# A four-layer graph kernel: the candidate's state product by seven block products, gates blocked by halves of the features, and new figures in its planner

## The chip, the cores and the metric

The kernel runs on one core of one Trainium2 chip, in one launch. The metric is the device time of that launch in microseconds. The core has TensorE (PE; its weight loads are shown apart as PEld), VectorE (DVE), ScalarE (ACT), GpSimd (POOL) and the DMA queues (SP is the queue that issues most loads). TensorE writes to PSUM, which has 8 banks of 128 x 512 fp32 here; the other data lie in SBUF. Everything is fp32.

## The reference

128 graphs of 64 nodes with 256 features pass through four residual layers, each followed by a layer norm. The change is in the first, a gated graph network of five steps with a GRU cell:

```python
for l in range(5):
    m = einsum('bnd,de->bne', h, weight[l])
    agg = einsum('bij,bid->bjd', A, m)          # A = (adj != 0)
    gi = agg @ w_ih.T + b_ih                    # split in i_r, i_z, i_n
    gh = h @ w_hh.T + b_hh                      # split in h_r, h_z, h_n
    r = sigmoid(i_r + h_r); z = sigmoid(i_z + h_z)
    n = tanh(i_n + r * h_n)                     # the candidate
    h = (1 - z) * n + z * h
x = layernorm(x + h * mask)
```

The second layer aggregates, goes from 256 to 1024 features, through an RMS norm and a SiLU, and back to 256; the third aggregates a tangent of the row and projects it onto a ball; the fourth is a small attention over the neighbours. Each is followed by its own layer norm.

## The kernel before

**Tiling.** Two graphs make a block of 128 rows, four blocks a group, and there are 16 groups. A group's state lies with the features on the partitions: `h[:, k, :]` is feature half k (128 features), and the 512 nodes of the group are cut into two halves n = 0, 1 of HR = 256 columns (`half(n)`). `agg` has the same form. The message weight is multiplied into the input weight ahead of time, so aggregation works on h itself.

**The gates** (`gated`, from line 716) are a product of [r; z] weights with [agg; h]. Written as a 2 x 2 block product, the blocks are r and z, agg and h, and the two halves of the nodes. The kernel uses the seven-product scheme (Winograd's form of Strassen's): `a11`, `a12`, `na22` and the weight sums `s1` to `s4` on one side, the sums `t1` to `t4` of values on the other, seven products of 256 x 256 x 256. One such product (`product`, line 656) is four matmuls of 128 x 256. So the gates take 28 matmuls per layer and group instead of 32. The sums t are four VectorE operations of 512 columns (`minus`, line 746), and mix agg with h.

**The candidate** has an input side (`p_in`, weights `w_in`, four matmuls for each half of the nodes) and a state side (`p_hn`, weights `w_hn`, four for each half, eight in all). The state side is computed in `sides(n)` together with the aggregation, and two operations for each half bring it to SBUF as `hnb`, scaled by 0.5 and with half its bias (`scaled`: ScalarE or VectorE). `new_n(n, t)` then makes the candidate of half n from `hnb`, r and `p_in`, and `new_state` the new state.

**The order.** Nothing is issued where it is written. Every operation is recorded in `Flow` with an engine, a booked duration, and what it reads and writes. `Plan.advance` walks a model of the engines, picks at each step the operation that can start first, and `Flow.issue` keeps the best of several plans and emits the instructions in that order; each engine then runs its instructions strictly in order. Operations of several groups stand side by side in it (`WINDOW` = 4 streams; most buffers exist for NF = 3 groups), so one group's matmuls fill another's waiting. The booked figures are:

```python
    HOPS = {"from PE": 0.25, "to PE": 0.3, "else": 0.1}          # L158, a crossing between engines
    def dve(n, run, w, r):
        flow.op("DVE", 0.16 + 0.00105 * n, run, w, r)            # L342
    def act(n, run, w, r):
        flow.op("ACT", 0.27 + 0.00077 * n, run, w, r)            # L345
```

An operation recorded by `either` (`copied`, `scaled`) may go to ScalarE or VectorE; line 99 chooses by start and by how much longer the slower engine takes. Reads and writes are recorded with a part, so `(ps, 0)` and `(ps, 1)` do not wait for each other in the plan. The semaphores themselves are placed by the layer below, from the order in which the instructions are emitted.

**Set-up** (lines 430 to 600) turns the weights, forms the products of the message weights with the input weights (`ps_wmih`), and the weight sums, for layer 0 on VectorE and for layers 1 to 4 on GpSimd.

Of the kernel before, what the change touches and what calls it, by code (L numbers as in the profile page):

```python
# [52 lines left out]
class Plan:  # L53
# [25 lines left out]
    def advance(self, until, rank):  # L79
# [3 lines left out]
        while self.left and clock["PE"] < until:  # L83
            best = None
            for s in range(self.first, min(self.first + flow.WINDOW, len(self.queues))):
                for e, q in self.queues[s].items():
                    opened = False
                    for _, o in zip(range(flow.AHEAD[e]), q):
                        t = max(clock[e], at[o.id])
                        if o.opens is not None:  # L90
                            if opened or not banks or need[o.id]:
                                opened = True
                                continue
                            t = max(t, banks[0])
                        elif need[o.id]:
                            continue
                        elif o.kb and e != "POOL":
                            t = max(t, self.lands[0])
                        key = (t + o.ways[e][0] - min(w[0] for w in o.ways.values()) if len(o.ways) > 1 else t, *rank(s, o))
                        if best is None or key < best[0]:  # L100
                            best = key, o, e, t
# [42 lines left out]
class Flow:  # L144
# [13 lines left out]
    HOPS = {"from PE": 0.25, "to PE": 0.3, "else": 0.1}  # L158
# [55 lines left out]
    def hop(self, e, to):  # L214
        if e == to:
            return 0.0
# [44 lines left out]
def kernel(  # L261
# [79 lines left out]
    def dve(n, run, w, r):  # L341
        flow.op("DVE", 0.16 + 0.00105 * n, run, w, r)  # L342

    def act(n, run, w, r):
        flow.op("ACT", 0.27 + 0.00077 * n, run, w, r)  # L345

    def copied(n, o, i, w, r):

        flow.either([("ACT", 0.27 + 0.00077 * n, lambda: nc.scalar.copy(o(), i())),  # L349
                     ("DVE", 0.16 + 0.00105 * n, lambda: nc.vector.tensor_copy(o(), i()))], w, r)  # L350

    def scaled(n, o, i, scale, bias, w, r):

        flow.either([("ACT", 0.27 + 0.00077 * n, lambda: nc.scalar.activation(o(), i(), AF.Identity, bias=bias(), scale=scale())),  # L354
                     ("DVE", 0.16 + 0.00105 * n, lambda: nc.vector.tensor_scalar(o(), i(), scale(), bias(), OP.mult, OP.add))], w, r)
# [62 lines left out]
    def gate_w(name):  # L418
        return fixed([P, KD, D], name)

    a12, na22, w_hn = gate_w("a12"), gate_w("na22"), gate_w("w_hn")
    a11, s1, s2, s3, s4, w_in = ([gate_w(f"{n}_{l}") for l in range(L)] for n in ("a11", "s1", "s2", "s3", "s4", "w_in"))

# [80 lines left out]
    def hh_out(i, k, ps):  # L504
        if i == 0:
            dve(256, lambda: nc.vector.tensor_copy(a12[:, k, :], ps[:, :D]), [(a12, k)], [ps])
            dve(256, lambda: nc.vector.tensor_scalar(na22[:, k, :], ps[:, D:], -1.0, None, OP.mult), [(na22, k)], [ps])
        else:
            dve(256, lambda: nc.vector.tensor_copy(w_hn[:, k, :], ps[:, :D]), [(w_hn, k)], [ps])
# [10 lines left out]
    for l in range(L):  # L520
# [9 lines left out]
        a21 = unit("AB"[l % 2], S, f"a21_{l}", (P, KD, D))  # L530
        for k in range(KD):
            for i, n in ((0, 2 * D), (1, D)):
# [5 lines left out]
                for dst, at in (((a11[l], 0), (a21, D)) if i == 0 else ((w_in[l], 0),)):  # L538
                    act(256, lambda ps=ps, k=k, dst=dst, at=at: nc.scalar.copy(dst[:, k, :], ps[:, at:at + D]),
                        [(dst, k)], [ps])  # L540

        def sums(e, us, l=l, a21=a21):
            v = nc.vector if e == "DVE" else nc.gpsimd
            for o, x0, x1 in ((s1[l], a21, na22), (s2[l], s1[l], a11[l]), (s3[l], a11[l], a21), (s4[l], a12, s2[l])):
                flow.op(e, us, lambda o=o, x0=x0, x1=x1: v.tensor_sub(o.tile(), x0.tile(), x1.tile()), [o], [x0, x1])
        sums("DVE", 0.7) if l == 0 else sums("POOL", 1.32)
# [5 lines left out]
    m11, m12, mn22, ms1, ms2, ms3, ms4 = range(7)  # L552
# [59 lines left out]
    def group(g):  # L612
# [104 lines left out]
        def gated(l, h):  # L717
# [5 lines left out]
            def sides(n):  # L723
# [5 lines left out]
                p_agg = aggregate(agg, hr, 2 * n, n)  # L729
                p_hn = bank("p_hn")  # L730
                product(p_hn, w_hn, lambda k: h[:, k, half(n)], True, True, (h, n))
                for c in range(KD):
                    scaled(300, lambda c=c: hnb[:, c, half(n)], lambda c=c: p_hn[:, c * HR:(c + 1) * HR], lambda: 0.5,
                           lambda c=c: half_b[:, 2 * KD + c:2 * KD + c + 1], [(hnb, (n, c))], [p_hn, half_b])
                return p_agg
# [3 lines left out]
            t1, t2, t3, t4 = (tA, 0), (tA, 1), (tB, 0), (tB, 1)  # L739
            a = agg  # L740

            def view(t):
                return t[0][:, t[1] * KD:(t[1] + 1) * KD, :]

            def minus(o, x0, x1, r):
                dve(512, lambda: nc.vector.tensor_sub(view(o), x0(), x1()), [o], r)  # L746

            def of(t, n):
                return lambda: t[:, :, half(n)]

            def k_of(t, n):
                return lambda k: t[:, k, half(n)]

            def k_view(t):
                return lambda k: t[0][:, t[1] * KD + k, :]
# [35 lines left out]
            sides(0)  # L791
            product(p1, a11[l], k_of(a, 0), True, False, (a, 0))
            copied(420, lambda: uu.tile(), lambda: blocks_of(p1.tile()), [uu], [p1])
            product(p_in[0], w_in[l], k_of(a, 0), True, True, (a, 0))
            product(p1, a12, k_of(h, 0), False, True, (h, 0))
            tanh_half(ur, lambda c: p1[:, c * HR:(c + 1) * HR], 0, p1)
            new_n(0, ur)
            p_a2 = sides(1)

            a2 = lambda: blocks_of(p_a2.tile())
            minus(t1, a2, of(a, 0), [p_a2, (a, 0)])
            minus(t2, of(h, 1), lambda: view(t1), [(h, 1), t1])
            minus(t3, of(h, 1), a2, [(h, 1), p_a2])
            minus(t4, lambda: view(t2), of(h, 0), [t2, (h, 0)])
            product(pu, s2[l], k_view(t2), True, True, t2)
            plus(uu, pu, uu)
            product(pv, s3[l], k_view(t3), True, False, t3)
            plus(uv, pv, uu)  # L810
            product(pw, s1[l], k_view(t1), True, False, t1)
            product(pv, na22, k_view(t4), False, True, t4)
            plus(uv, pw, uv)
            plus(uz, pv, uu)
            product(pw, s4[l], k_of(h, 1), False, True, (h, 1))
# [4 lines left out]
            product(p_in[1], w_in[l], k_of(a, 1), True, True, (a, 1))  # L820
# [166 lines left out]
        dve(1250, series, [n2, ser, near], [xn])  # L987
# [4 lines left out]
        for b in range(NB):  # L992
            flow.either([
                ("DVE", 0.37, lambda b=b: nc.vector.tensor_scalar(tan[:, b, :], x2[:, b, :], fac[:, b:b + 1], None, OP.mult)),
                ("ACT", 0.47, lambda b=b: nc.scalar.activation(tan[:, b, :], x2[:, b, :], AF.Identity, scale=fac[:, b:b + 1]))],
# [29 lines left out]
        dve(800, onto_ball, [th, un], [th, un, urn])  # L1025
# [14 lines left out]
        for b in range(NB):  # L1040
            ps = bank("ps_a")
            for k in range(KD):
# [5 lines left out]
                ("ACT", 0.47, lambda ps=ps, b=b: nc.scalar.activation(  # L1048
                    hw[:, b, :D], ps[:, :D], AF.Identity, scale=hw[:, b, D:D + 1])),
                ("DVE", 0.43, lambda ps=ps, b=b: nc.vector.tensor_scalar(  # L1050
# [52 lines left out]
```

## Time and profile before

| | |
|---|---|
| time, median of 3 | 2431.84 us (2430.58 to 2432.48) |
| span of the profiled run | 2430.5 us, granted TensorE clock 0.994 |
| TensorE busy | 2394.7 us, 12,258 matmul records |
| VectorE busy | 1893.4 us, 4,097 instructions |
| ScalarE busy | 1147.1 us, 2,408 instructions |
| GpSimd busy | 188.2 us |
| `p_hn` matmuls (state side) | 1,280 records |
| `hnb` from PSUM, on ScalarE / VectorE | 232 x 472 ns / 88 x 480 ns |
| HBM traffic | 25.74 MB read, 8.39 MB written |

An fp32 matmul of 128 x 256 stands as two records in the trace, so records are twice the program's matmuls for that shape. A row of the page names the output and inputs by the program's names without their numbers (`p_w<-tA,s` is a product of a t sum with an s sum). The page's "idle before" is the time an engine stood ahead of the instructions of a row, with what released it.

### The profile page before, as it was taken

The page shows a single profiled execution, that of the slowest core. Times are in us where ns is not written, and L with a number is a line of the kernel's source. Part 1 is how long each engine was busy: PE and PEld are TensorE (multiplying, and loading weights), DVE is VectorE, ACT ScalarE, POOL GpSimd, SP SyncE. Part 2 cuts the span into 40 slices and gives each one's busy share as a digit, 9 for nine tenths or more (in the row PEclk, how much of TensorE's full clock was granted, in tenths as well). Part 3 has the DMA queues.
Part 4 walks back from the last instruction along what each step waited for, and adds up shares of the span by engine and source line. Part 5 has one row for each costly group of instructions (what it writes and reads, how often), then busy time and mean ns, then how long its engine had stood idle before and what let it go on. Part 6 is the DMA issues. An engine that isn't in the chain of part 4 may idle for free.

```text
span 2430.5 us, 32703 instructions
## 1 busy us (share of the span) xinstructions
PE 2394.7 (99%) x12258; PEld 2102.9 (87%) x12258; DVE 1893.4 (78%) x4097; ACT 1147.1 (47%) x2408; POOL 188.2 (8%) x144
## 2 busy tenths in 40 slices
PE   9999999999999999999999999999999999999995
PEld 7888888888888888888888888888888888888864
DVE  3668787887888877778777887888787787878777
ACT  4434544444444444454444545455444544445453
POOL 4000000000100000000000100000000000000011
PEclk9999999999999999999999999999999999999997
DMA  4000000000000000000000000000000000000000
GB/s 127 3 1 12 1 29 1 18 12 1 29 1 27 3 18 11 1 27 3 16 14 1 29 1 27 3 19 11 1 29 1 18 12 1 27 9 18 9 9 18
DMA packets 39725, 36.21 MB, mean 15 GB/s; under 512 B 9956, under 2 KB 38656, under 8 KB 39568
## 3 DMA queue, kind: packets, MB, share of 16 engines
q1 hardware_dynamic: 37840, 32.25, 4.2%
q8 instruction: 97, 1.59, 0.3%
q10 hardware_dynamic: 1328, 1.31, 0.2%
q0 software_dynamic: 400, 0.57, 0.1%
q14 instruction: 60, 0.49, 0.1%
HBM read 25.74 MB, written 8.39 MB: 14 GB/s over the span
## 4 chain that ended last, share of the span: by engine, by line
PE 94%; DVE 4%; ACT 1%; DMA 1%; issue 0%; POOL 0%; SPq 0%; POOLq 0%; ACTq 0%; DVEq 0%
PE p_v L663 11%; PE p_w L663 11%; PE p_in L663 11%; PE p_r L663 11%; PE p_hn L663 11%; PE ps_o L333 9%; PE ps_agg L333 6%; PE p_u L663 6%; PE ps_hr L643 3%; PE ps_a L333 2%; PE p_wh L882 2%; PE p_vh L882 2%; PE p_1h L882 2%; PE ps_T L633 1%; PE ps_att L333 1%; PE p_uh L882 1%
## 5 line engine op out<-in xcount | busy, mean ns | idle before, releaser
L663 PE MATMUL p_hn<-hT,w_hn 128*128 128x256 f32 x1280 | 322.8, 380 | 0.0
L663 PE MATMUL p_in<-agg,w_in 128*128 128x256 f32 x1280 | 315.4, 379 | 0.0
L663 PEld LDWEIGHTS p_in<-agg,w_in 128*128 128x128 f32 x1280 | 240.2, 190 | 31.1
L663 PEld LDWEIGHTS p_hn<-hT,w_hn 128*128 128x128 f32 x1280 | 227.9, 191 | 22.7
L333 PE MATMUL ps_o<-w2s,hid 128*128 128x256 f32 x1024 | 231.2, 379 | 0.0
L333 PEld LDWEIGHTS ps_o<-w2s,hid 128*128 128x128 f32 x1024 | 193.9, 190 | 27.3 <-issue 1.2
L678 POOL TENSOR_TENSOR rstd<-ve,pow 128x4 f32<-128x4 f32 (+1 forms) x64 | 82.5, 1289 | 1491.6 <-DVE ve L676 1484.0
L767 ACT ACTIVATE V<-V,half_b 128x256 f32<-128x256 f32 x160 | 72.7, 500 | 199.2 <-DVE V L763 199.0
L663 PE MATMUL p_u<-tA,s 128*128 128x256 f32 x640 | 158.1, 381 | 1.4 <-DVE tA L746 0.6
L663 PE MATMUL p_w<-tA,s 128*128 128x256 f32 x640 | 158.1, 379 | 0.0
L663 PE MATMUL p_r<-hT,a 128*128 128x256 f32 x640 | 156.9, 379 | 0.0
L663 PE MATMUL p_r<-agg,a 128*128 128x256 f32 x640 | 156.7, 379 | 0.0
L663 PE MATMUL p_v<-tB,s 128*128 128x256 f32 x640 | 155.4, 379 | 0.0
L663 PE MATMUL p_v<-tB,na 128*128 128x256 f32 x640 | 154.5, 379 | 0.0
L663 PE MATMUL p_w<-hT,s 128*128 128x256 f32 x640 | 154.3, 379 | 0.0
L349 ACT COPY agg<-ps_agg 128x512 f32<-128x512 f32 x154 | 89.9, 584 | 114.2 <-PE ps_agg L333 98.8
L333 PEld LDWEIGHTS ps_agg<-edge,hr 128*128 128x128 f32 x1024 | 136.1, 191 | 6.6
L354 ACT ACTIVATE hnb<-p_hn,half_b 128x256 f32<-128x256 f32 x232 | 101.6, 472 | 81.4 <-PE p_hn L663 67.4
L333 PE MATMUL ps_agg<-edge,hr 128*128 128x128 f32 x1024 | 138.8, 275 | 0.0
L663 PEld LDWEIGHTS p_u<-tA,s 128*128 128x128 f32 x640 | 119.3, 190 | 21.0 <-DVE tA L746 2.3
L663 PEld LDWEIGHTS p_v<-tB,s 128*128 128x128 f32 x640 | 120.9, 190 | 16.3 <-PE ps_att L333 0.2
L663 PEld LDWEIGHTS p_w<-hT,s 128*128 128x128 f32 x640 | 120.7, 190 | 16.0
(233 smaller groups left out, 4686.5 us busy)
## 6 DMA issues: line engine op xcount, KB each, us to landing
x<-in_x_dram SPq DMA_DIRECT2D x16, 512.0 KB, 3.6
xr<-in_x_dram SPq DMA_DIRECT2D x16, 512.0 KB, 3.6
out_dram<-x_n SPq DMA_DIRECT2D x16, 512.0 KB, 2.9
edge<-in_adj_dram SPq DMA_DIRECT2D x32, 64.0 KB, 2.3
wm<-in_L_gnn_weight_dram SPq DMA_DIRECT2D x5, 256.0 KB, 5.3
w2s<-in_L_gnn_W_dram SPq DMA_DIRECT2D x1, 1024.0 KB, 10.0
w<-in_L_gnn_W_dram SPq DMA_DIRECT2D x2, 512.0 KB, 3.5
w_in_L_gnn_w_hh_dram<-in_L_gnn_w_hh_dram ACTq DMA_DIRECT2D x1, 512.0 KB, 5.2
```

The source lines that it names most:

```text
L333: return nc.tensor.matmul(o, lhsT, rhs, start=(k == 0), stop=(k == nk - 1))
L349: flow.either([("ACT", 0.27 + 0.00077 * n, lambda: nc.scalar.copy(o(), i())), ("DVE", 0.16 + 0.00105 * n, lambda: nc.vector.tensor_copy(o( ...
L354: flow.either([("ACT", 0.27 + 0.00077 * n, lambda: nc.scalar.activation(o(), i(), AF.Identity, bias=bias(), scale=scale())), ("DVE", 0.16 ...
L633: turn(lambda j=j, c=c: nc.tensor.transpose(ps[:, c * HR + j * P:c * HR + (j + 1) * P], src[:, 2 * n + j, c * P:(c + 1) * P], ident.tile() ...
L643: turn(lambda j=j, c=c: nc.tensor.transpose(ps[:, j * D + c * P:j * D + (c + 1) * P], src[:, c, (2 * n + j) * P:(2 * n + j + 1) * P], iden ...
L663: pe(256, lambda c=c, k=k: nc.tensor.matmul(ps[:, c * HR:(c + 1) * HR], w[:, k, c * P:(c + 1) * P], v(k), start=first and c == k == 0, sto ...
L678: pool(1.1, lambda: nc.gpsimd.tensor_tensor(rstd[:, :m, :], ve[:, :m, :], pow2[:, :m, :], OP.pow), [rstd], [ve])
L767: act(256, lambda c=c: nc.scalar.activation(o[:, c, :], src(c), AF.Tanh, bias=half_b[:, i * KD + c:i * KD + c + 1], scale=0.5), [(o, c)], ...
L882: pe(256, lambda c=c: nc.tensor.matmul(ps[:, c * HR:(c + 1) * HR], w1f[:, w, (2 * q + c) * P:(2 * q + c + 1) * P], v[0](), start=first and ...
```

## The change

There are three parts.

1. **The state side by seven block products.** The weights `w_hn` (256 x 256) are kept as seven 128 x 128 blocks: four blocks (`m11`, `m12`, `mn22` with its sign turned, and one that is overwritten by the fourth sum) and the sums `ms1` to `ms4`, all scaled by 0.5 already. The values are cut by feature half and node half, and the sums `t1` to `t4` of h alone. Seven matmuls take the place of eight. They share two banks, `p_hx` and `p_hy`, in two halves each, and are joined in SBUF by VectorE: two sums with what is in `hs`, and three outputs with sum and bias in one operation.
2. **The gates are blocked by halves of the features.** In the 2 x 2 form the inner blocks are now the feature halves k, each with both agg and h, in place of agg and h. A product is still four matmuls, two from h (`w_h`) and two from agg (`w_a`). For that the sums are formed on h and agg apart: eight of 256 columns in place of four of 512. The sums of h are the ones that the state side needs. Because the sums of h need both halves of the state, and the outputs for node half 0 come partly at the end of the seven, `new_n(0)` now follows the whole of `state_side`.
3. **The planner's figures.** Booked durations of VectorE and ScalarE come down, crossings go up, an operation that follows another on its own engine is booked with a crossing too, and an operation that may go to either engine is booked on VectorE only with 0.4 us added to its start in the comparison.

```diff
-                        key = (t + o.ways[e][0] - min(w[0] for w in o.ways.values()) if len(o.ways) > 1 else t, *rank(s, o))
+                        key = (t + flow.SOONER if len(o.ways) > 1 and e == "DVE" else t, *rank(s, o))
...
-    HOPS = {"from PE": 0.25, "to PE": 0.3, "else": 0.1}
+    HOPS = {"from PE": 0.3, "to PE": 0.3, "else": 0.2, "own": 0.12}
+    SOONER = 0.4
...
-            return 0.0
+            return 0.0 if e == "PE" else self.HOPS["own"]
...
-        flow.op("DVE", 0.16 + 0.00105 * n, run, w, r)
+        flow.op("DVE", 0.105 + 0.00105 * n, run, w, r)
...
-        flow.op("ACT", 0.27 + 0.00077 * n, run, w, r)
+        flow.op("ACT", 0.15 + 0.00077 * n, run, w, r)
...
-    a12, na22, w_hn = gate_w("a12"), gate_w("na22"), gate_w("w_hn")
-    a11, s1, s2, s3, s4, w_in = ([gate_w(f"{n}_{l}") for l in range(L)] for n in ("a11", "s1", "s2", "s3", "s4", "w_in"))
+    m11, m12, mn22, ms1, ms2, ms3, ms4 = range(7)
+    w_h, w_hn = fixed([P, 7, D], "w_h"), fixed([P, 7, P], "w_hn")
+    w_a, w_in = [fixed([P, 7, D], f"w_a_{l}") for l in range(L)], [fixed([P, KD, D], f"w_in_{l}") for l in range(L)]
+    def sums_of(w, eng, us):
+        for o, x0, x1 in ((ms1, ms4, mn22), (ms3, m11, ms4), (ms2, ms1, m11), (ms4, m12, ms2)):
+            flow.op(eng, us, lambda o=o, x0=x0, x1=x1: v.tensor_sub(w[:, o, :], w[:, x0, :], w[:, x1, :]),
...
-                p_hn = bank("p_hn")
-                product(p_hn, w_hn, lambda k: h[:, k, half(n)], True, True, (h, n))
-                for c in range(KD):
-                    scaled(300, lambda c=c: hnb[:, c, half(n)], lambda c=c: p_hn[:, c * HR:(c + 1) * HR], lambda: 0.5, ...
+            def sums(x, i):
+                for o, x0, x1 in ((of(t1), at(0, 1), at(0, 0)), (of(t2), at(1, 1), of(t1)),
+                                  (of(t3), at(1, 1), at(0, 1)), (of(t4), of(t2), at(1, 0))):
+                    dve(256, lambda o=o, x0=x0, x1=x1: nc.vector.tensor_sub(o[0](), x0[0](), x1[0]()), ...
+            def gate(ps, m, v, first, last):
+                for i, w in ((1, w_h), (0, w_a[l])):
+                    for c in range(KD):
+                        pe(256, lambda i=i, w=w, c=c: nc.tensor.matmul(
+                            ps[:, c * HR:(c + 1) * HR], w[:, m, c * P:(c + 1) * P], v[i][0](), ...
+            def state_side():
+                px, py = bank("p_hx"), bank("p_hy")
+                prod(px, 0, m11, block(0, 0), True)
+                copied(256, su[0], lambda: px[:, :HR], [su[1]], [(px, 0)])
+                prod(px, 0, m12, block(1, 0))
+                scaled(256, out(0, 0)[0], lambda: px[:, :HR], lambda: 1.0, lambda: b(0), [out(0, 0)[1]], [(px, 0), half_b])
+                prod(px, 1, ms2, sum_of(t2))
+                plus(su, px, 1, su)
+                prod(py, 0, ms3, sum_of(t3), True)
+                plus(sv, py, 0, su)
+                prod(py, 1, ms1, sum_of(t1))
+                prod(py, 0, mn22, sum_of(t4))
+                plus(out(0, 1), py, 0, su, 1)
+                plus(out(1, 1), py, 1, sv, 1)
+                prod(py, 1, ms4, block(1, 1))
+                plus(out(1, 0), py, 1, su, 0)
...
-            sides(0)
-            product(p1, a11[l], k_of(a, 0), True, False, (a, 0))
+            agg_of(0)
+            gate(p1, m11, block(0, 0), True, False)
             copied(420, lambda: uu.tile(), lambda: blocks_of(p1.tile()), [uu], [p1])
-            product(p1, a12, k_of(h, 0), False, True, (h, 0))
+            gate(p1, m12, block(1, 0), False, True)
             tanh_half(ur, lambda c: p1[:, c * HR:(c + 1) * HR], 0, p1)
+            sums(h, 1)
+            state_side()
+            product(p_in[0], w_in[l], lambda k: agg[:, k, half(0)], True, True, (agg, 0))
             new_n(0, ur)
-            p_a2 = sides(1)
-            minus(t1, a2, of(a, 0), [p_a2, (a, 0)])
+            agg_of(1)
+            sums(agg, 0)
...
-        dve(1250, series, [n2, ser, near], [xn])
+        dve(1150, series, [n2, ser, near], [xn])
```

Some fixed bookings of single operations (`series`, `onto_ball`, `tan`, `hw`) change in the same way; what they compute does not.

## The prediction

> **What bounds the kernel now.** I read the page's busy shares first, then the chain of waits that ended last, then a table of stretches, and last a few microseconds of the timeline.
>
> ```profile
> PE 2394.7 (99%) x12258; PEld 2102.9 (87%) x12258; DVE 1893.4 (78%) x4097; ACT 1147.1 (47%) x2408; POOL 188.2 (8%) x144
> ...
> PE 94%; DVE 4%; ACT 1%; DMA 1%; issue 0%; POOL 0%; SPq 0%; POOLq 0%; ACTq 0%; DVEq 0%
> ...
> L663 PE MATMUL p_hn<-hT,w_hn 128*128 128x256 f32 x1280 | 322.8, 380 | 0.0
> ```
>
> TensorE is busy for 99% of the span and 94% of the closing chain runs over it. The state's product for the candidate (p_hn) never waits: its last column, idle before, is 0.0. The other products of line 663 show 0.0 too, or 1.4.
>
> ```profile
> core 0: us, PE busy (x) PEld busy (x) DVE busy (x) ACT busy (x) POOL busy (x), PEclk, DMA share, GB/s
> ...
> 400.00:1000.00 600.00, 599.29 (x3111) 532.62 (x3110) 484.35 (x1045) 283.67 (x596) 42.74 (x29) 1.00 0.04 12
> ...
> 2300.00:2430.50 130.50, 101.00 (x414) 73.84 (x413) 99.45 (x277) 62.63 (x125) 18.58 (x13) 0.88 0.04 13
> ```
>
> In the body TensorE stands 0.7 us of 600 at full clock; nearly all its idle time is in the last 130 us (29.5) and the first 61 (3.4). Busy time can hide gaps, since records overlap, so I read the pitch:
>
> ```profile
> 2311.04 1.89 PE L663 MATMUL p_u<-tA,s 128*128 128x256 f32 x8
> ...
> 2312.77 1.89 PE L663 MATMUL p_v<-tB,s 128*128 128x256 f32 x8
> 2312.97 0.69 DVE L763 TENSOR_TENSOR U<-p_u,U 128x512 f32<-128x512 f32 x1 [1.07 <-PE p_u L663]
> ...
> 2314.50 1.89 PE L663 MATMUL p_w<-tA,s 128*128 128x256 f32 x8
> ```
>
> Eight records are four matmuls of the program (two records each: p_hn has 1280 records for 16 groups x 5 layers x 8 matmuls). They start 1.73 us apart, so one 128x256 matmul takes 1.73 / 4 = 0.432 us of TensorE, not the 0.380 of one record. I went through all start-to-start steps and took off the shortest of each shape: 38.7 us are left over, 4.2 in the first 61 us, 22.2 in the last 122 and 12.3 in the 2,250 between. The kernel is bound by TensorE's issue, and a matmul removed from the body is worth its pitch.
>
> **What the Trainium skill says.** "Perfetto Trace Analysis", section Identifying the Most-Contended Engine, says that matmul busy time is no good measure of headroom and to use the weight loads' busy share. Here that is 87%, not 99%; the pitch explains it, since a load takes 0.190 us in a step of 0.216. The same page, Engine Utilization, halves TensorE's rate for fp32 done as low and high parts; the two records per matmul agree. The page "PSUM — Partial Sum Buffer", section PSUM bank collisions, says that two engines must not touch the same bank in the same partitions at once, whichever columns they use, so that their accesses have to be ordered by bank. The trace shows such ordering: two evictions of different halves of one p_hn bank wait for each other,
>
> ```profile
> ACT hnb L354 <- DVE hnb L355: 13.0, 16, 2.7
> ...
> DVE hnb L355 <- ACT hnb L354: 8.5, 20, 1.3
> ```
>
> 36 times and 21.5 us in all. This matters below: the new code keeps two products in the two halves of one bank, and the planner books those halves apart.
>
> **The change, part by part.** Counts come from the two built programs, engine by engine.
>
> *TensorE.* The state side goes from 8 matmuls of 128x256 per layer and group to 7: 80 layers (16 x 5) lose one each, 6,676 to 6,596 in all. 80 x 0.432 = **34.6 us**. The gates stay at 28 matmuls a layer; they are only cut another way, and each still loads its own weights, 0.190 hidden under a step of 0.216. Rows of equal instructions rise from 2,538 to 3,394 because gate products now alternate between w_h and w_a; nothing in the timeline charges for a change of weights, so I take 0.
>
> *VectorE.* Removed: 320 sums of 512 (the four tA/tB groups of line 746: 59.4 + 57.9 + 54.9 + 54.5 = 226.7 us) and 88 evictions of hnb (88 x 0.480 = 42.2). Added: 640 sums of 256, nearest the page's line 878 at 0.42 us (268.8); 160 sums of 256 out of PSUM, not seen before: below them 0.42 (line 959's eviction), above 0.48 (line 1028), I take 0.42 (67.2); 240 sums with a bias column, 0.42 to 0.48, I take the upper, as hnb took it (115.2). Net +182. The planner now starts an either-engine operation on VectorE only if that is 0.4 us sooner, and the program shows what moves to ScalarE: 120 x_n (x 0.409), 28 hr (x 0.69), 40 tan (x 0.29), 27 hw (x 0.484), some 9 copies of 512 (x 0.69): −99. VectorE goes to about 1,976 us, 82% of the new span.
>
> *ScalarE.* Loses 232 hnb (101.6), gains 80 at 0.47, 79 copies of 256 at 0.375, the 120 x_n at 0.55, 40 tan at 0.47, 27 hw at 0.47 and 36 copies at 0.58: about +84, to 1,231 us or 51%. Neither engine is full; beside TensorE this costs nothing unless it comes late.
>
> *New waits on TensorE.* The seven products come back three times to a bank that has just been read: m12 after the copy, mn22 after su becomes sv, ms4 after the output of line b(1). Such a return takes from TensorE's last step to VectorE's start 0.20 us (2312.77 to 2312.97 above), 0.42 to 0.48 for the operation, and about 0.06 back (a tA sum that ended at 1655.79 let p_u start at 1655.85): 0.70 us. What stands behind a waiting matmul is all of TensorE's queue, so a late one costs its lateness in full. What hides it is other groups' work placed between by the planner, which books 0.6 us for the two crossings and is aware of these three. It is not aware of the bank: its parts (px, 0) and (px, 1) are free of each other, yet the program's semaphores order them. Counting in the program's order, 297 matmuls into p_hx or p_hy follow a read of the other half; 52 have about 1 us of matmuls or less between, where a return takes 0.70 or more when VectorE is not free at once. At 0.1 us each I take **5 us**; bounds 0 and 30 (all 297 at 0.1). Some 370 VectorE reads also wait for a matmul into the other half, up to 0.43 us each; VectorE's free 18% takes that up.
>
> *Edges.* In the last two layers of the last group there is little else to place between the returns: six returns, a third of a microsecond each, **2 us**. The tail of 22.2 us has the same shape in both programs (two groups side by side, then tan, x3T and attention), 0. Set-up: the sums of w_h and w_hn are eight VectorE operations of 0.4 us or less, and the program puts transposes and the weight products there, 0. The sums of w_a on GpSimd are half the size of before and were not waited for, 0.
>
> *Longer chain per layer.* new_n for half 0 now waits for the last of the seven products, some five returns of 0.70 + 0.43: 5.7 us a layer, 28 a group. Three sets of buffers are in flight, so a group lives about 3 x 2431 / 16 = 456 us for 2,376 / 16 = 148 us of TensorE work; 300 us of its life are waiting that others fill. Cost 0.
>
> *Planner's numbers.* Durations come down to what the timeline shows between starts (VectorE 512: 0.643 booked, 0.60 to 0.72 seen; ScalarE 256: 0.347 booked, 0.41 seen between two tanh), and crossings go up. Neither sign is clear: 0, with −12 (all body gaps filled) and +18 as bounds.
>
> Sum: −34.6 + 5 + 2 = −27.6; 2431.8 − 27.6 = **2404**.
>
> **Rivals.**
> 1. *The planner's new numbers also close gaps.* For: 12.3 us of gaps in the body and 22 in the tail are there to be won. Against: most gaps hang on single chains. −34.6 − 10: 2387.
> 2. *Late evictions.* VectorE's idle time falls from 537 to about 430 us, ScalarE's booked times are short by 0.06 a piece, and the bank ordering is unbooked, so gaps of the body more than double: −34.6 + 18 + 2: 2417.
> 3. *Returns become the bound; slower.* If a third of the 240 planned returns (3 x 80) meet an unfinished operation and wait out a full 0.70: 56 us, and 2431.8 − 34.6 + 56 = 2453. For it: the unbooked bank ordering and a fuller VectorE. Against: in the body even the sums that feed p_u make TensorE wait only 0.6 us in 2,430.
>
> **How the numbers follow.** Forecast 0.61, rival 1 0.12, rival 2 0.19, rival 3 0.08. The time is the forecast's, 2404. The range runs from 2388 (near rival 1) to 2424 (past rival 2, within the 30 us bound on bank waits), leaving out rival 3 and half of rival 1. Slower than 2436.7 has 0.06 of rival 3, within 0.2% its remaining 0.02; faster 0.92.
>
> **What would show it.** Right: 160 fewer matmul records; TensorE still 98 to 99% busy, with a 0.216 us step; idle before p_hx and p_hy of a few microseconds in all; VectorE near 1,976 us with sums of 256 at 0.42 us; a tail alike. Wrong: tens of microseconds of TensorE idle released by VectorE or ScalarE before p_hy, p_hx, p_u or p_r; a stretch of the body with TensorE under 98%; a tail longer by over 5 us; or a granted clock under 1.00 in the body.

## The result, and the profile after

The changed kernel takes **2455.88 us** (median of 4, 2455.07 to 2458.01) against 2432.01 us before: ratio 1.0101, 95% interval [1.0083, 1.0118]. It is 24 us slower, 52 us above the forecast and outside the range.

From the page of the changed kernel, the rows that answer to those shown of before:

```profile
PE 2387.4 (97%) x12098; PEld 2071.0 (84%) x12098; DVE 1884.3 (77%) x4516; ACT 1206.0 (49%) x2561; POOL 171.8 (7%) x144
...
PE 88%; DVE 6%; ACT 3%; issue 1%; DMA 1%; POOL 0%; POOLq 0%; ACTq 0%; DVEq 0%
...
L791 DVE SCALAR_TENSOR_TENSOR hnb<-p_hy,half_b,hs 128x256 f32<-128x256 f32 x240 | 110.9, 478 | 66.7 <-PE p_hy L780 65.4
...
L780 PE MATMUL p_hy<-tA,w_hn 128*128 128x256 f32 x480 | 136.7, 388 | 11.7 <-DVE tA L756 6.8
```

TensorE has its 160 records fewer, yet fell from 99% to 97%, and the share of the closing chain that is TensorE from 94% to 88%: other engines' operations now stand in it. VectorE is no fuller than before. And p_hy has an idle column that is not zero, released by VectorE. The stretches show where:

```profile
400.00:1000.00 600.00, 596.24 (x3077) 525.61 (x3076) 481.42 (x1154) 309.89 (x649) 42.53 (x30) 1.00 0.04 12
1000.00:1600.00 600.00, 586.78 (x2993) 512.34 (x2991) 465.69 (x1096) 295.73 (x632) 35.41 (x26) 0.99 0.04 12
...
2300.00:2454.40 154.40, 123.58 (x526) 93.37 (x524) 101.52 (x299) 81.43 (x162) 18.03 (x14) 0.92 0.03 11
```

The first number after the length is TensorE's busy time. The body, where 0.7 us of 600 were idle, loses 3.8 and 13.2 us in the two stretches of 600.

Start-to-start steps, added up as in the prediction, split the 23.9 us by which the profiled spans differ:

| | before | after |
|---|---|---|
| matmuls at their shortest step | 2375.6 | 2341.0 |
| gaps between matmuls | 38.7 | 100.3 |
| of these, first 61 us | 4.2 | 5.1 |
| body | 12.3 | 65.7 |
| tail (last 125 us) | 22.2 | 29.5 |
| before the first and after the last matmul's start | 16.2 | 13.1 |

So the expected 34.6 us came (160 records fewer at an unchanged step); 61.6 us of new gaps took them and more. A small part of the gaps is no waiting: the trace has the granted clock at half in five short stretches of the changed kernel (38 us, two of them in the body, at 1387.5 and 1602.5) and in three of the kernel before (33 us, all in the tail). From the steps that took twice their time there I estimate 10 of the 100.3 us and 5 of the 38.7. By the matmul that stands behind the gap, p_hy has 31.6 us and p_hx 7.1 (p_hn had 0.9), ps_sup 17.6 (9.2), ps_agg 10.3 (3.7), p_vh 3.1 (0.0). The waits of the changed kernel, longest in total (engine, who waited, for whom: us, times, longest):

```profile
PEld p_hy L780 <- DVE hnb L791: 27.6, 47, 1.5
...
DVE tA L756 <- DMA out_dram<-x_n: 21.4, 6, 4.1
...
PE ps_sup L336 <- ACT tan L1048: 13.2, 8, 9.5
...
PE p_hy L780 <- DVE hnb L791: 9.2, 25, 1.1
```

The first, second and fourth of these lead to two causes that the plan does not know. **The other half of a bank**, in the timeline of the changed kernel:

```profile
1320.93 1.03 PE L780 MATMUL p_hy<-tA,w_hn 128*128 128x256 f32 x4
...
1321.79 1.03 PE L672 MATMUL p_in<-agg,w_in 128*128 128x256 f32 x4
1321.99 0.42 DVE L789 TENSOR_TENSOR hs<-p_hy,hs 128x256 f32<-128x256 f32 x1 [0.44 <-PE p_hy L780]
1322.46 0.48 DVE L791 SCALAR_TENSOR_TENSOR hnb<-p_hy,half_b,hs 128x256 f32<-128x256 f32 x1
1322.99 0.30 PEld L780 LDWEIGHTS p_hy<-tA,w_hn 128*128 128x128 f32 x2 [0.57 <-DVE hnb L791]
1322.99 0.70 PE L780 MATMUL p_hy<-tA,w_hn 128*128 128x256 f32 x2 [0.17 <-DVE hnb L791]
```

The first four records are ms3 and ms1, into halves 0 and 1 of p_hy. The sum that reads half 0 starts only 0.20 us after both (two matmuls of 0.432 from 1320.93 end at 1321.79), so it waited for the half that it doesn't read. The next matmul, mn22, adds to half 0, whose reader was done at 1322.41; it starts at 1322.99, when the reader of half 1 has ended (1322.94). p_in's two matmuls ended at 1322.65, so 0.34 us of TensorE are lost, and 0.10 more right after it: the second record of mn22 starts 0.32 us after the first in place of 0.216, as it does after some seventy stops in this trace. This very gap, 0.33 to 0.34 us between p_in and mn22, stands in the trace twelve times.

The planner, run again on this kernel's text, gives the order of all operations, and with it which read each waiting matmul stood behind. Of the gaps before p_hy and p_hx, 23.6 us (51 matmuls, 0.46 us each, the 0.10 after the stop included) were ended by a read of the other half, 2.1 us (5) by a read of the matmul's own half, which the plan books, and 11.5 us by sums of h that came late. The rest is under 2 us.

**The store of the output**, further up in the same timeline:

```profile
1289.83 0.38 SPq L1118 DMA_DIRECT2D out_dram<-x_n  x1
...
1291.62 0.47 ACT L357 ACTIVATE hnb<-p_hx,half_b 128x256 f32<-128x256 f32 x1 [0.28 <-PE p_hx L780]
1293.02 0.76 DVE L756 TENSOR_TENSOR tA<-hT 128x256 f32<-128x256 f32 x2 [4.11 <-DMA out_dram<-x_n]
...
1293.84 0.70 PE L780 MATMUL p_hy<-tA,w_hn 128*128 128x256 f32 x2 [2.25 <-DVE tA L756]
```

tA shares its buffer with x_n, the finished output of the group that used the same set three groups ago. The plan books the store at 0.1 us; the trace lets it land after 2.9. In the kernel before the t sums needed aggregates of both halves and came late in the layer; the sums of h come as soon as h is there. TensorE loses 2.4 us here, and 11.0 us in five such places (three of 2.4 us, and 2.1 and 1.7; 11.5 us with the slower steps after the stops). The sixth wait of tA for the store, 1.9 us at 2125.9, holds no state matmul. TensorE does lose 2.6 us soon after it, before a p_vh, but the store had landed by then; a sum of 256 columns ahead on VectorE took 2.58 us in place of 0.42 there, and what held it is not known. The expectations below still count six places and 13.5 us.

### The profile page after: what moved, and what is told of

Same layout as the page of the kernel before. It is cut to its first block, busy times and chain, and to the rows that moved or that the text cites. A ratio compares the mean times of both kernels' runs of the same rounds, so it can differ in the third digit from the quotient of the medians.

```text
span 2454.4 us, 33052 instructions
## 1 busy us (share of the span) xinstructions
PE 2387.4 (97%) x12098; PEld 2071.0 (84%) x12098; DVE 1884.3 (77%) x4516; ACT 1206.0 (49%) x2561; POOL 171.8 (7%) x144
## 4 chain that ended last, share of the span: by engine, by line
PE 88%; DVE 6%; ACT 3%; issue 1%; DMA 1%; POOL 0%; POOLq 0%; ACTq 0%; DVEq 0%
PE p_v L769 11%; PE p_w L769 10%; PE p_r L769 10%; PE p_in L672 9%; PE ps_o L336 9%; PE ps_agg L336 6%; PE p_hy L780 6%; PE p_u L769 5%; PE p_hx L780 4%; PE ps_hr L652 3%; PE ps_a L336 2%; PE p_vh L935 2%; PE p_wh L935 2%; PE p_1h L935 2%; DVE hnb L791 1%; PE ps_sup L336 1%
## 5 line engine op out<-in xcount | busy, mean ns | idle before, releaser
L769 PE MATMUL p_v<-tB,w_a 128*128 128x256 f32 x640 | 172.1, 379 | 0.0
L769 PE MATMUL p_v<-tA,w_h 128*128 128x256 f32 x640 | 169.8, 380 | 0.7 <-DVE V L819 0.7
L769 PE MATMUL p_r<-hT,w_h 128*128 128x256 f32 x640 | 167.9, 381 | 0.0
L769 PE MATMUL p_r<-agg,w_a 128*128 128x256 f32 x640 | 166.6, 379 | 0.0
L791 DVE SCALAR_TENSOR_TENSOR hnb<-p_hy,half_b,hs 128x256 f32<-128x256 f32 x240 | 110.9, 478 | 66.7 <-PE p_hy L780 65.4
L780 PE MATMUL p_hy<-tA,w_hn 128*128 128x256 f32 x480 | 136.7, 388 | 11.7 <-DVE tA L756 6.8
L769 PEld LDWEIGHTS p_v<-tB,w_a 128*128 128x128 f32 x640 | 120.8, 190 | 16.1
L769 PEld LDWEIGHTS p_r<-agg,w_a 128*128 128x128 f32 x640 | 119.6, 190 | 16.3 <-ACT agg L352 0.6
L769 PEld LDWEIGHTS p_v<-tA,w_h 128*128 128x128 f32 x640 | 116.6, 190 | 15.3 <-DVE V L819 1.3
L769 PEld LDWEIGHTS p_r<-hT,w_h 128*128 128x128 f32 x640 | 116.4, 191 | 13.7 <-ACT U L352 0.4
```

The source lines that it names most:

```text
L769: pe(256, lambda i=i, w=w, c=c: nc.tensor.matmul(ps[:, c * HR:(c + 1) * HR], w[:, m, c * P:(c + 1) * P], v[i][0](), start=first and i == 1 ...
L780: pe(256, lambda: nc.tensor.matmul(ps[:, j * HR:(j + 1) * HR], w_hn[:, m, :], v[1][0](), start=first, stop=True, skip_group_check=True), [ ...
L791: dve(300, lambda: nc.vector.scalar_tensor_tensor(o[0](), ps[:, j * HR:(j + 1) * HR], b(c), x[0](), OP.add, OP.add), [o[1]], [(ps, j), x[1 ...
```

## The experiments

Eighteen kernels, each measured beside the kernel before. The theories at the start: **B**, TensorE waits for the bank whose halves the plan books apart; **O**, sums wait for a store that the plan takes for short; **F**, the planner's new figures give a worse order, whatever the instructions; **G**, the gates' new cut costs time. C, J, P and T come up with their runs. Each run is one order of the planner; how far an order alone moves the time is measured at the end (some 14 us either way), and single differences below that are not read as effects. TensorE's steps sum to 2375.6 us in those with eight state matmuls and to 2341.0 in those with seven.

**Which part: figures or instructions.** e1_old_figures is the changed kernel with every figure of the planner put back; e2_new_figures is the kernel before with the new ones.

```diff
-    HOPS = {"from PE": 0.3, "to PE": 0.3, "else": 0.2, "own": 0.12}
+    HOPS = {"from PE": 0.25, "to PE": 0.3, "else": 0.1}
...
-        flow.op("DVE", 0.105 + 0.00105 * n, run, w, r)
+        flow.op("DVE", 0.16 + 0.00105 * n, run, w, r)
```

> The changed kernel with the planner's figures of before (crossings, booked durations, the choice between ScalarE and VectorE). Measured so far: the changed kernel starts its matmuls 34.6 us faster in sum (2341.0 against 2375.6 us of pitch), and has 61.6 us more of gaps between them (100.3 against 38.7). Theory F (the figures book too little time, so that evictions come late everywhere): the gaps of the body fall from 66 back to some 20 us, about 2410 us. Theory B (the two halves of the banks p_hx and p_hy are booked as free of each other, while the semaphores order them): some 25 us of gaps before p_hy and p_hx stay, 2440 to 2456 us. Theory O (the sums of h go into a buffer from which the output of an earlier group is still being stored, and the planner books that store at 0.1 us): six waits of about 2.3 us stay whatever the figures.

Measured: 2495.8 us (1.0264 [1.0249, 1.0279]), 40 us slower than the change. Theory F falls: the old figures are no help to the new instructions. Gaps before p_hy and p_hx stay (36.3 us; 26.0 behind reads of the other half, 6.2 behind late sums of h), as B and O said, and others come, at ps_rms (18.1), p_v (11.3), ps_ss (10.0).

> The kernel before with the planner's figures of the change, nothing else. Theory F: slower than before by 25 to 35 us, about 2460. Theories B and O: no shared bank halves and no early write into the stored buffer here, so within 8 us of 2432; what it is slower by is the part of the figures alone, in the tail (ps_sup) above all.

Measured: 2450.0 us (1.0075 [1.006, 1.009]), between the two expectations: 18 us slower than before, 15.4 of it in gaps of the body. None of them is before p_hn.

**The two unbooked waits.** e3_banks books the state's banks whole; e4_out books the store as the 512 KB that it is; e5_banks_out does both. The instructions are those of the changed kernel, but for a few that go to the other of two engines; their order is another.

```diff
-                        [(ps, 0), (ps, 1)] if first else [(ps, j)], [(w_hn, m), v[1][1]])
+                        [ps], [(w_hn, m), v[1][1]])
...
-        flow.op("SP", 0.1, lambda: nc.sync.dma_start(out_rows[g], o.tile()), (), [o])
+        flow.op("SP", 0.1, lambda: nc.sync.dma_start(out_rows[g], o.tile()), (), [o], kb=512)
```

> The changed kernel with the two state banks booked whole, so that the planner knows every wait that the semaphores make; same instructions, another order. Theory B: the gaps before p_hy and p_hx fall from 38.7 to about 15 us (11 of them theory O's), about 2432 us. Theory F: within 6 us of 2456.

Measured: 2417.56 us (0.9943 [0.9928, 0.9958]), 38 us less than the change and faster than the kernel before. Gaps before p_hy and p_hx: 9.1 us, of which 0.4 stand behind a read of the other half and 6.5 behind the three store waits that this order has. The time is 14 us below what theory B expected.

> The changed kernel with the store of the output booked as a transfer of 512 KB in place of 0.1 us; same instructions, another order. Theory O: the waits of the tA sums for the store (21.4 us of VectorE, about 13.5 us of TensorE in six places) go, about 2442 us. Theories B and F: they account for the rest, so no less than 2438; if the store costs nothing in the end, 2456.

Measured: 2427.67 us (0.9984 [0.9978, 0.9991]). The wait of the tA sums for the store is gone from the list; the time fell by 28 us where 13.5 were expected, below the floor of 2438 that B and F set. p_hy keeps 19.0 us and p_hx 2.6, of which 19.1 stand behind reads of the other half. The 28 us are thus more than the store; part of them is another order.

> The changed kernel with both corrections to the plan: state banks booked whole and the store of the output booked as a transfer. Each alone took 38 and 28 us off. Theory B and O as two causes: e3 still has about 11 us of TensorE waits behind the store, so 2417.6 - 11 = 2407 us, and gaps before p_hy and p_hx under 5 us. Theory J (any re-ordering of the plan gives a few tens of microseconds by chance, and neither correction is a cause): anywhere from 2417 to 2440.

Measured: **2408.98 us** (0.9904 [0.9888, 0.9921]), as B and O said. Its TensorE waits:

```profile
PE ps_sup L336 <- ACT tan L1048: 11.0, 6, 9.5
PE ps_hr L652 <- DVE hT L844: 3.6, 2, 3.0
...
PE p_hy L780 <- DVE hnb L791: 0.4, 1, 0.4
```

p_hy, 9.2 us in 25 waits in the change, waits once. Gaps of the body fell from 65.7 to 18.1, those before p_hy and p_hx to 2.2. The page of this kernel:

```profile
PE 2370.0 (98%) x12098; PEld 2076.6 (86%) x12098; DVE 1878.8 (78%) x4514; ACT 1211.8 (50%) x2563; POOL 177.2 (7%) x144
```

**The bank itself.** e6_own_banks gives each of the four running sums a bank of its own, with the store booked.

```diff
-                px, py = bank("p_hx"), bank("p_hy")
+                px, py = ((bank(t), bank(t)) for t in ("p_hx", "p_hy"))
```

> The changed kernel with each of the four running sums of the state side in a bank of its own (four of eight banks for a while in place of two), parts booked as they are, and the store booked as a transfer. Theory B: the waits for the other half's reader are gone on the chip itself, so gaps before p_hy and p_hx under 6 us; 2427.7 (store booked, halves shared) - 20 = 2408. Rival P (eight banks are too few for this): the new waits for a free bank show before p_u, p_v, p_in or ps_agg, and the time is 2420 or more.

Measured: 2413.84 us (0.9924 [0.9909, 0.9939]). Gaps before p_hy and p_hx are 0.8 us. Beside the changed kernel's 27.6 us in 47 waits, the same row reads

```profile
PEld p_hy L780 <- DVE hnb L791: 0.2, 1, 0.2
```

No wait for a bank shows before p_u, p_v, p_in or ps_agg: B holds on the chip, P doesn't. That avoiding the shared bank is worth more than booking it can't be told from these runs.

**The gates alone.** e7_gates_only keeps the new gates and figures and puts the eight state matmuls back, one bank for each half of the nodes.

```diff
-            state_side()
...
+                product(p_hn, w_hn, lambda k: h[:, k, half(n)], True, True, (h, n))
```

> The changed kernel without its first part: gates blocked by halves of the features and new figures, but the state side as before in eight matmuls with one bank for each half of the nodes. Theories B and O: no half-bank is shared, so no gaps before p_hn; the early tA sums still meet the store (some 10 us); with 34.6 us more of matmuls than the change. e2 (old gates, same figures) took 2450, so 2450 to 2462. Theory G (the blocking of the gates itself costs, by 64 VectorE columns more a layer in smaller pieces): over 2470, with gaps before p_u, p_v and p_w.

Measured: 2444.02 us (1.0048 [1.0033, 1.0063]), 6 us below e2, which has the old gates and the same figures, and 6 us below what was expected. Cutting the gates by features costs nothing that can be told; G falls. The wait for the store is not in its list, against the expectation: early sums meet it in some orders and not in others.

**What is left in the figures.** Turns of e5. e8_booked_act books ScalarE's operations 0.06 to 0.12 us longer, as the trace has them:

```diff
-        flow.op("ACT", 0.15 + 0.00077 * n, run, w, r)
+        flow.op("ACT", 0.21 + 0.00077 * n, run, w, r)
...
-        flow.either([("ACT", 0.15 + 0.00077 * n, lambda: nc.scalar.activation(
+        flow.either([("ACT", 0.27 + 0.00077 * n, lambda: nc.scalar.activation(
```

> As e5_banks_out, with ScalarE's operations booked nearer to what the traces show between starts (256 columns: 0.41 from SBUF, 0.47 with a scale and bias, tan and hw 0.43, in place of 0.347 and 0.37). Theory F in what is left of it: late x_n, tan and hw on ScalarE make some 20 us of the gaps before ps_agg, ps_T, ps_sup; with true figures 5 to 10 us less than e5. Otherwise within 5 us of e5 either way.

Measured: 2421.28 us (0.9954 [0.994, 0.9969]), 12 us slower than e5, which is within the chance of an order; a new wait of TensorE for hid takes 9.6 us. That longer bookings for ScalarE help, by 5 to 10 us, is not seen.

e9_old_figures_booked is e5 with all of the old figures (the diff of e1); e15_old_crossings takes only the old crossings (HOPS, and none between two operations of one engine), e16_old_durations only the old durations.

> As e5_banks_out (2409.0), with all of the planner's figures of before. Of the old gates the new figures cost 18 us (e2: 2450.0 against 2432.0); in the change they save 40 (e1: 2495.8 against 2455.9). Theory C (the 40 came from the wrong bookings, which loose figures made worse): with banks and store booked, the old figures are the better ones, about 2391. Theory T (seven products with returns need the longer crossings and the crossing on an engine's own queue): slower than e5 whatever is booked, 2430 or more, with gaps spread over p_v, p_r, ps_rms, ps_ss as in e1.

Measured: 2444.66 us (1.0053 [1.0038, 1.0068]). Theory T: with p_hy down to 0.7 us, the gaps are at ps_rms (16.6), ps_T (14.7), ps_o (11.2), p_v (7.8).

> As e5_banks_out (2409.0), with the crossings of before (0.25, 0.3, 0.1 and none on an engine's own queue) and the new durations. e9 with all old figures took 2444.7. If the crossings are what the seven products need (their returns run over two of them): 2430 to 2445. If it is the durations (the old ones book VectorE at 0.16 + 0.00105 n, which with 4,513 instructions fills it to over 90% of the plan): within 8 us of 2409.

Measured: 2500.32 us (1.0284 [1.0269, 1.03]).

> As e5_banks_out, with the durations of before and the new crossings and choice. The counterpart of e15: if the over-full VectorE of the plan is the cause of e9's gaps (ps_rms, ps_o, p_v, ps_T), 2430 or more; if the crossings, within 8 us of 2409.

Measured: 2444.77 us (1.0058 [1.0043, 1.0073]). The expectations took it for one or the other; the two act together. With banks and store booked, new crossings and new durations give 2409.0, old durations 2444.8, old crossings 2500.3, and both old (with the old choice) 2444.7. Short durations with short crossings are the worst. There the gaps before p_hy and p_hx are back at 29.0 us although their banks are booked whole, 15.4 behind reads of the other half and 9.3 behind reads of the own half:

```profile
PEld p_hy L780 <- DVE hs L789: 16.4, 30, 1.2
...
PEld p_hy L780 <- DVE hnb L791: 9.8, 14, 1.6
```

So booking a bank whole was enough only where the booked return was long enough too (e5, e9 and e16 against e15). Nothing is left in the plan of e15 for the 0.05 us that the trace shows between two dependent VectorE operations (1322.41 to 1322.46 above) and for the 0.42 us that a sum booked at 0.374 takes. That this is the reason is argued, not shown.

e10_old_choice is e5 with the old choice between engines:

```diff
-                        key = (t + flow.SOONER if len(o.ways) > 1 and e == "DVE" else t, *rank(s, o))
+                        key = (t + o.ways[e][0] - min(w[0] for w in o.ways.values()) if len(o.ways) > 1 else t, *rank(s, o))
```

> As e5_banks_out, with the old rule of choice between ScalarE and VectorE (by the difference of booked durations in place of 0.4 us against VectorE). If the leaning on ScalarE is what makes x_n and tan late (waits before ps_sup, ps_T and ps_agg of some 28 us in e5, 20 in the kernel before), about 2400; if not, within 6 us of 2409.

Measured: 2411.23 us (0.9914 [0.9898, 0.9931]): the choice between ScalarE and VectorE is worth nothing that can be told.

The longest single wait left in e5 is ps_sup's 9.5 us for tan in the tail. The timeline of the changed kernel, ScalarE alone, shows what stands ahead of tan there:

```profile
2415.50 1.28 ACT L1065 ACT_TABLE_LOAD   x1
2416.80 0.20 ACT L1065 ACTIVATE th<-n 128x4 f32<-128x4 f32 x1
2417.02 1.28 ACT L1028 ACT_TABLE_LOAD   x1
2418.31 0.20 ACT L1028 ACTIVATE fac<-fac 128x4 f32<-128x4 f32 x1
2420.13 1.31 ACT L1048 ACTIVATE tan<-x_n,fac 128x256 f32<-128x256 f32 x3 [1.61 <-DVE fac L1043]
```

A tanh and a logarithm each bring in their table, 1.28 us for an operation of 0.20. The two loads fill 2.6 us of the 9.5. A larger part, 4.7 us, passes before small GpSimd and VectorE operations have worked out what the logarithm reads (at 2415.84, where ps_sup stood from 2411.19). The plan has the logarithm's load booked (2600 columns) and not the tanh's (64). e11_table_load is e5 with both booked:

```diff
-        act(64, lambda: nc.scalar.activation(th.tile(), unb.tile(), AF.Tanh), [th], [unb])
+        act(1700, lambda: nc.scalar.activation(th.tile(), unb.tile(), AF.Tanh), [th], [unb])
```

> As e5_banks_out, with the small tanh of the third layer booked at 1.46 us, the table load of 1.28 us that the trace shows ahead of it included, in place of 0.20. In the kernel before the last group's logarithm runs before that tanh and ps_sup waits 3.0 us for tan; in the change it runs after it, behind two table loads, and ps_sup waits 9.5. If the booking is what puts the tanh first: the 9.5 us wait falls to about 3, 2402 us; if the order is chance: within 5 us of 2409.

Measured: 2410.12 us (0.9909 [0.9894, 0.9924]). The last group's logarithm runs ahead of the tanh there and brings in no table of its own, the 9.5 us wait is gone (the longest of ps_sup for tan is 4.2), and the tail's gaps fell from 32.8 to 23.4 us, but the body's rose from 18.1 to 26.4. The order at the end did follow the booking; the time did not move.

**How much is the chance of one order.** The same bookings, with one number of the search turned (LAG 40 to 45 or 35). It weighs how far a group may run ahead against how long its remaining work is, and touches no duration.

```diff
-    WINDOW, STRETCH, WIDTH, LAG = 4, 25.0, 8, 40.0
+    WINDOW, STRETCH, WIDTH, LAG = 4, 25.0, 8, 45.0
```

> As e5_banks_out, with one number of the planner's search changed (LAG 45 in place of 40) and no booking touched: what a mere re-ordering is worth. Theory J: differs from 2409 by 10 us or more. Otherwise within 6 us, and the 38, 28 and 47 us of the two corrections are no chance.

> The changed kernel with LAG 45 in place of 40 in the planner's search, no booking touched. Is 2456 what the change costs, or partly a chance of the order? In e12 the same turn took 6.4 us off. Theories B and O: the waits before p_hy and for the store are made by bookings that stay wrong, so 2440 to 2465, with 20 us or more of gaps before p_hy. Theory J: under 2430.

> The kernel before with LAG 45: how lucky the order was that the change is measured against. If the old figures serve the old instructions well in general: within 8 us of 2432. If 2432 was a lucky order: 2440 to 2455, and then the 18 us of e2 are no cost of the new figures.

> The changed kernel with LAG 35: a third order from the same bookings (40: 2455.9, 45: 2441.2). If the unbooked waits set the level, 2438 to 2460 with 20 us or more of gaps before p_hy; if one of the two was an outlier of the search, anything down to 2420.

> The kernel before with LAG 35: a third order of the old program (40: 2432, 45: 2442.6). If 2432 is a lucky one, 2438 to 2448 here too; if 2442.6 is the unlucky one, 2428 to 2436.

e12 moved by 6.4 us, just past its bound. e13 came within its range, with 27.8 us of gaps before p_hy and p_hx. e17 did not: its gaps are there (22.4 us), its time is 9 us below the range. e14 and e18 disagree on 2432; of the three orders of the kernel before, 2442.6 is the one apart.

| bookings | LAG 40 | LAG 45 | LAG 35 | gaps before p_hy and p_hx |
|---|---|---|---|---|
| kernel before | 2432.0 | 2442.6 (e14) | 2430.7 (e18) | none |
| change | 2455.9 | 2441.2 (e13) | 2429.0 (e17) | 38.7, 27.8, 22.4 |
| change, banks and store booked | 2409.0 (e5) | **2402.6** (e12) | not run | 2.2, 3.6 |

e12's ratio is 0.9877 [0.9863, 0.9892], the fastest kernel of the study. e17's is 0.9989 [0.9982, 0.9996]. One order is worth some 14 us either way. So the 24 us between the two programs are not the worth of the change: over three orders the change averages 2442.0 and the kernel before 2435.1, within their spread. What does not drown in the spread is the third row: 33 to 36 us below the change's average (2442.0 to 2409.0 or to the pair's 2405.8), and the gaps before p_hy and p_hx in every order of the second row. Of these, a read of the other half ended 23.6, 25.4 and 18.9 us; in e13, for instance:

```profile
PEld p_hy L780 <- DVE hnb L791: 25.2, 45, 1.3
```

The store is another matter. The sums of h wait for it six times in the change, five in e1 and three in e3, but once in e17 (2.7 us; 2.3 us of TensorE, before a ps_hr, come right after) and never in e13, with the same booking of 0.1 us. The gaps before p_hy and p_hx of e13 are 10.9 us shorter than the change's, of 14.7 us in time. The timeline shows the wait; whether an order meets it is chance. The slowest of the two orders of the third row is 20 us faster than the fastest of the second, and 22 faster than the fastest of the kernel before. The kernel before was not run with its store booked; its lists show no wait for it but 0.5 us in e14.

The single effects of e3 (38) and e4 (28), which add up to more than e5's 47, contain such chance.

## Why the prediction was wrong, point by point

- *34.6 us from 80 matmuls*: right. 2375.6 to 2341.0, and the step stayed at 0.216 us a record. Rows alternating between w_h and w_a, and the gates' new cut: 0, and no cost shows (e7 against e2).
- *New waits on TensorE, 5 us*: **the term that failed first.** The mechanism was named, the shared bank with halves booked apart, and its size was wrong. I had counted in the program's order 52 of 297 matmuls with little between and given each 0.1 us; 51 waited for a read of the other half, for 0.46 us each, 23.6 us in all (18.9 to 25.4 over three orders). Whether they are the same matmuls was not looked at. So the number of waits came out right, which may be luck, and the length of one was more than four times what I had booked for it. The plan lays other matmuls only where it sees a wait, and a VectorE read held back by the other half's matmul (0.43 us in the example) makes the next return late as well. I had written that VectorE's free time takes that up; the example shows the two chained. The three returns that the plan knows were hidden, as forecast: 2.1 us. The 21.5 us that I had read as bank waits in the kernel before were idle times of up to 2.7 us that ended so, longer than one eviction of 0.48, so not all of them was the bank.
- *Nothing for stores*: a step that was missing. I had checked what the change adds and not what it brings forward: sums that start earlier meet a buffer whose last reader is a transfer. 11.5 us in this order, none in e13 and up to 2.3 in e17; the transfer's 2.9 us and its booking of 0.1 were both there to be read before.
- *Planner's numbers, 0 with −12 and +18*: too narrow. The order's chance alone is 12 us (before) and 27 us (change) from end to end in three tries, and the new figures with the old gates cost 18 (of which some may be chance too: 2450.0 against 2430.7 to 2442.6).
- *Edges, 2 us*: 8.2 in gaps (start +0.9, tail +7.3), partly given back by an end 3.1 us shorter outside the gaps. I had put the tail at 0; the wait of 9.5 us for tan in it, two table loads included, had not been foreseen.
- *VectorE to 1,976 us, 82%*: wrong, 1,884 and 77%. The added operations cost about what was said (hnb 110.9 us for 115.2), and the durations of all VectorE operations add up to 71 us more than before, for 83 forecast. But independent operations of 256 run into each other: two sums take 0.76 us in the store's lines above, not 0.84. Busy time counts an overlap once, and the overlap grew by 80 us, from 173 to 254. ScalarE: 1,206 for 1,231.
- *Rival 3*, slower, 2453: it gave the time, at 0.08, by returns that meet an unfinished operation; true for some 26 of its 56 us. That its time came out is luck: the rest is the store, the tail and the order, and other orders of the same change took 2441.2 and 2429.0.
- *What would show it wrong* held: idle released by VectorE before p_hy, a body under 98%, a tail longer by over 5 us, and a granted clock under 1.00 in the body (0.99 in the second stretch of 600).

With the waits booked the change takes 2409.0 and 2402.6, around the 2404 forecast. That does not make the prediction right: it was made for the plan that books the halves apart and the store at 0.1 us.

## What to carry to other kernels

Where a planner orders the instructions and a lower layer places the semaphores, compare what both take for a dependency before anything else: a wait that the plan does not book is paid on the engine that bounds, and booking two of them was worth about as much (33 to 36 us) as the matmuls saved (34.6). When a change makes work ready earlier, look who still reads the buffer it goes to, transfers above all. And before a difference of one per cent between two planned orders is read as the worth of an edit, turn a number of the search that means nothing and see how far the time moves.

## What the runs showed of the hardware that was not expected

- Accesses of two engines to different halves of one bank wait for each other in both directions: a read 0.43 us for a matmul into the half it doesn't read, a matmul 0.34 us for a reader of the other half. The trace puts these waits down to semaphores; the sum itself takes no longer (0.42 us in the example).
- A stop of TensorE costs more than the wait: the step after it was 0.32 us in place of 0.216 some seventy times in the changed kernel.
- A return from TensorE through VectorE costs 0.20 us, the operation's 0.42 to 0.48, and 0.05 back (1322.94 to 1322.99), as the prediction had it.
- Each change between tanh and logarithm on ScalarE costs a table load of 1.28 us. With the second load booked the planner put the logarithm first, and the 9.5 us wait of ps_sup for tan was gone (e11).
